# Layer 0's pairs: copying the last product with its bias on ScalarE and adding the residual in one sum

## The chip, the cores and the metric

The kernel runs on one core of a Trainium2 chip. The metric is the device time of one launch in microseconds (us), as the median of several runs. Profiles are of one execution of the same kernel. The engines are named as in the profile: PE (matrix products; PEld is its weight load), DVE (VectorE), ACT (ScalarE), POOL (GpSimd), and SP, which here only issues DMAs. [...]

## The reference, cut to what matters

Sixteen batches of 256 x 256 values pass through two residual layers. Each batch has a router row of eight numbers.

```python
# layer 0: one expert of 8 for each batch, with biases
e = argmax(cond_8, axis=-1)
h = silu(x @ W_up[e].T + b_up[e]) * (x @ W_gate[e].T + b_gate[e])     # 256 -> 512
x = x + (h @ W_down[e].T + b_down[e])                                 # 512 -> 256, residual
# layer 1: the two best experts for each batch, and a shared one; no biases
y = gelu(x @ shared_gate) * (x @ shared_up) @ shared_down             # 256 -> 1024 -> 256
for each of the two experts e with weight w:
    y += w * (gelu(x @ gate[e]) * (x @ up[e]) @ down[e])
x = x + y
```

The change concerns the last line of layer 0: the product with `W_down`, its bias `b_down` and the residual `x`.

## The kernel before, in words

**Units.** Batches are sorted by expert at run time. Two batches with the same expert make a `Pair`, one left over makes a `Single`. In layer 0 there are a first single, one more single, four pairs that always exist (`l0_pairs`), and up to three further pairs or the singles in their place, chosen at run time by a switch. In layer 1 there are the eight shared pairs and the routed ones. The kernel is written with an order by hand: no scheduler moves an instruction within an engine's queue.

**A pair's products** are done as 2 x 2 block products with seven multiplications in place of eight (the list `STEPS`). They need sums of blocks on both sides. On the weight side POOL makes four sums per matrix in `sums_a` (L479 to L482): `sums_q` for each quarter of the first matrices (tile `s`), `sums_d` for the last matrix (tile `ds`). On the activation side DVE makes three instructions in `sums_b` (L472 to L474), for the input `x` (tile `bt` in layer 0, `xt` in layer 1) and for the hidden activations (also in a `bt`). In layer 0 the second of these sums of `x` lies in a `dz` buffer.

**First matrices (`up`, L541).** For each quarter `j`, PE runs the seven products into PSUM banks X, Y and Q. ACT copies X to SBUF (`copy`, L522, tile `cp`), and DVE adds or subtracts Y or Q to or from the copy (`combine`, L526, tile `c`). Then ACT applies the functions: in layer 0 SiLU and an identity, each with bias, in `act0` (L571), in layer 1 the GELU (L577). DVE multiplies the two halves (L580, tile `bt`), and `sums_b` follows. A layer 0 pair has two quarters, a layer 1 pair four.

**Last matrix (`down`, L597).** The seven products go to banks A (for X), B (for Q) and Y. Each of the four result blocks C11, C12, C22, C21 has an `early` and a `late` half. `early` takes the content of A out into a `dz` buffer. In layer 0 that is one DVE instruction which adds the bias column and the block of x (L614). In layer 1 it is an ACT copy with a scale (L619), or for the very last pair a DVE sum (L612). `late` then combines the `dz` buffer with bank Y or B on DVE into the result tile `ys` (L630 where no routing weight is applied). The order in `down` is: after product 0 `early` C11; 1: `late` C11; 2: `early` C12; 4: `early` C22 and C21, `late` C22; 5: `late` C21; 6: `late` C12, and the pair's buffers are given back. Product 2 accumulates into the same bank A that product 0 wrote, so it can start only when the `early` of C11 has read it; product 4 stands likewise behind the `early` of C12.

**Order of the work.** `Line` has a clock that advances with every pair product. `later(after, f)` puts a step off by so many ticks, and `flush` runs what is due. The products of a pair's last matrix are put off and fall among the first products of the next pair. `ahead` runs at the start of each quarter: it loads q five quarters ahead, makes the POOL sums of the first matrices three quarters ahead (`sums_q`), loads the last matrix, and in layer 0 puts that matrix's POOL sums (`sums_d`) off by 12 ticks. A quarter has six products of two ticks each, so 12 ticks is just the next quarter's start.

**Stores.** When a pair is done, `done` records its store and `send` issues it at the start of the next quarter. In layer 0 each of the two batches goes from `ys` to the DRAM tensor `x1d`, from which layer 1 loads its input, and to `out`; both are SP DMAs (L453, L454). `x1d` of the first pair is what layer 1's first shared pair loads into `xt`.

Of the kernel before, what the change touches and what calls it, by code (L numbers as in the profile page):

```python
# [10 lines left out]
AF = mybir.ActivationFunctionType  # L11
ALU = mybir.AluOpType
# [47 lines left out]
def kernel(  # L60
# [10 lines left out]
    nc = tc.nc  # L71
# [40 lines left out]
    def take(tag, *shape, of=None):  # L112

        i = turns[tag].pop(0)
        if tag not in HELD:
            turns[tag].append(i)
        else:
            assert (tag, of) not in turns
            turns[tag, of] = i
        t = rings[tag][i]  # L120
        n = 1
        for d in shape:
            n *= d
        t = t[:, :n]
        if len(shape) == 1:
            return t
        names = "abcd"[: len(shape)]
        return t.rearrange(
            f"p ({' '.join(names)}) -> p {' '.join(names)}", **dict(zip(names, shape))
        )  # L130

    def when_free(tag, f):

        if turns[tag] and not turns["later", tag]:
            f()
        else:
            turns["later", tag].append(f)

    def give(tag, of):
        turns[tag].append(turns.pop((tag, of)))  # L140
        if turns["later", tag]:
            turns["later", tag].pop(0)()

    def bank(tag):
        return take(tag, N2)
# [311 lines left out]

    class Pair(Unit):
        width, last = 2, False
        first, step = 18, None  # L460


# [124 lines left out]
        def down(self, k):  # L587

            tag, a, b = STEPS[k]
            if k == 0:  # L590
                self.ys = take("ys", KD, 2, S, of=self)
            if OPENS[k]:
                self.banks[tag] = bank({"X": "A", "Q": "B", "Y": "Y"}[tag])
            src = self.d[:, A_AT[a]] if a in A_AT else self.ds[:, S_AT[a]]
            d = self.banks[tag][:, :S]
            for j in range(self.kp):
                nc.tensor.matmul(  # L597
                    d,
                    lhsT=src[:, j, :],
                    rhs=self.acts[j][:, B_AT[b], :],  # L600
                    start=OPENS[k] and j == 0,
                    stop=j == self.kp - 1,
                    skip_group_check=True,
                )

            def early(block):
                c, t = block % 2, block // 2
                e = take("dz", S, of=(self, block))
                self.copies[block] = e
                src = self.banks["X"][:, :S]  # L610
                if self.last:
                    nc.vector.tensor_tensor(e, self.z[:, c, t, :], src, ALU.add)  # L612
                elif not self.layer:
                    nc.vector.scalar_tensor_tensor(  # L614
                        e, src, self.bd[:, c : c + 1], self.xt[:, block, :], ALU.add, ALU.add
                    )
                else:
                    w = 1.0 if self.at is None else self.weight(t)
                    nc.scalar.activation(e, src, AF.Copy, scale=w)  # L619

            def late(block, tag, sign):
                c, t = block % 2, block // 2
                e, src = self.copies[block], self.banks[tag][:, :S]
                dst = self.ys[:, c, t, :]
                if self.layer and self.at is not None:
                    nc.vector.scalar_tensor_tensor(  # L626
                        dst, src, self.weight(t, sign), e, ALU.mult, ALU.add
                    )
                else:
                    nc.vector.tensor_tensor(dst, e, src, ALU.add if sign > 0 else ALU.subtract)  # L630
                if self.last:
                    queue = (nc.sync, nc.scalar)[t]
                    store = queue.dma_start(self.out[t][:, c, :], dst)
                    for other in self.stores[1 - t]:
                        tc.declare_no_dep(store.ins, other.ins, reason="another batch")
                    self.stores[t].append(store)
                give("dz", (self, block))

            if k == 0:
                early(C11)  # L640
            elif k == 1:
                late(C11, "Y", 1)
            elif k == 2:
                early(C12)
            elif k == 4:
                early(C22)
                early(C21)
                late(C22, "Q", -1)
            elif k == 5:
                late(C21, "Y", 1)  # L650
            elif k == 6:
                late(C12, "Q", -1)
                give("d", self)
                for j in range(self.kp):
                    give("bt", (self, j))
                if not self.layer:
                    give("bt", self)
                if not self.last:
                    self.done(self.ys)
# [123 lines left out]
    l0_pairs = [Pair(next(names), 0, 2 * i) for i in range(NP1)]  # L783
# [4 lines left out]
    pairs = [Pair(next(names), 1, 2 * i) for i in range(NP2)]  # L788
    more_pairs = [Pair(next(names), 1, 2 * NP2 + 2 * i) for i in range(MOST[1])]
    ones = [Single(next(names), 1, 2 * NP2 + i) for i in range(NS2)]  # L790
    shared[-1].last = True
    shared[-2].step = 7

# [38 lines left out]
    class Line:  # L832
# [24 lines left out]
        def ahead(self, i):  # L857

            at = dict(enumerate(quarters))
            if i + Q_AHEAD in at:  # L860
                u, j = at[i + Q_AHEAD]
                u.load_q(j)
            if i + S_AHEAD in at:
                u, j = at[i + S_AHEAD]
                if u.width == 2:
                    when_free("s", lambda u=u, j=j: u.sums_q(j))
                if j == 0:
                    if u.width == 2 and not u.layer:
                        when_free("bt", u.load_x)
                    else:  # L870
                        if u.layer:
                            self.send(0)
                        u.load_x()
            if i + 1 in at:
                u, j = at[i + 1]
                if u.width == 2 and j == 0:

                    self.later(5 if i > 1 and at[i][0].width == 2 else 0, u.sums_x)
                    self.flush(self.clock)
            if i < 0:  # L880
                return
            u, j = at[i]
            pair0 = u.width == 2 and not u.layer
            if j == 0 and u is not l0_first:
                if u.d_from in HELD:
                    when_free(u.d_from, u.load_d)
                else:
                    u.load_d()
            if pair0 and j:
                self.later(12, u.sums_d)  # L890
            elif u.width == 2 and j == 2:
                u.sums_d()
            if u is shared[-1] and j == 2:
                u.load_z()
# [206 lines left out]
```

## Time and profile before

| what | value |
|---|---|
| median of 3 runs | 1051.06 us (1050.55 to 1051.47) |
| the profiled execution's own time | 1051.36 us |
| its span, first to last instruction | 1049.7 us |
| granted PE clock | 0.999 |
| PE busy, whole span | 1038.2 us |
| DVE busy, whole span | 777.0 us |
| DVE busy from 82 to 112 us (layer 0's pairs) | 28.89 of 30 us |
| ACT busy in the same stretch | 13.11 of 30 us |
| POOL busy in the same stretch | 19.16 of 30 us |
| L614 from 40 to 120 us | 14 instructions, 467 to 485 ns each |

The profile times are of a single execution, in us from the span's start. A row `ys<-dz,Y` reads: writes tile `ys`, from tile `dz` and PSUM bank Y. In a list of waits, each row tells which engine waited at which line for which, the total, the number of waits and the longest. A wait is put down to the release that came last by the profile, which can be a coincidence. In a timeline, the number in brackets is the idle time of the engine ahead of the instruction.

### The profile page before, as it was taken

To read this page: it belongs to the slowest core of one execution; us is meant where nothing else is said; L and a number is where in the kernel's file an instruction comes from. 1 tells how busy PE (TensorE), PEld (TensorE's weight loads), DVE (VectorE), ACT (ScalarE), POOL (GpSimd) and SP (SyncE) were. 2 spreads that over 40 slices of the span, in tenths; PEclk is the share of its full clock that TensorE was granted. 3 is DMA by queue.
4 is the path that set the end of the run, shared out by engine and by line. 5 is a ranking of instruction groups with operands and counts; after the bars stand their busy time and mean duration, and the time that the engine had idled before them with its cause. 6 is when DMAs were issued, how large, how long until landed. Compare 5 with 4: busy or idle time off the path is not lost.

```text
span 1049.7 us, 14152 instructions
## 1 busy us (share of the span) xinstructions
PE 1038.2 (99%) x4750; PEld 900.3 (86%) x4750; DVE 777.0 (74%) x1207; ACT 371.3 (35%) x583; POOL 446.7 (43%) x492
## 2 busy tenths in 40 slices
PE   9999999999999999999999999999999999999998
PEld 6778888888888888888888888888888888888886
DVE  7789978878687877887777778777766236776764
ACT  2444353535333333333333333333333123333331
POOL 2946331221043765666476556645201245630000
PEclk9999999999999999999999999999999999999999
DMA  7636656656664355345335533543655445356522
GB/s 237 241 127 203 240 181 194 207 166 236 200 235 119 88 140 140 93 109 140 98 87 138 140 98 103 140 122 83 178 159 171 133 136 156 91 180 184 183 75 45
DMA packets 60974, 157.47 MB, mean 150 GB/s; under 512 B 7506, under 2 KB 27090, under 8 KB 56658
## 3 DMA queue, kind: packets, MB, share of 16 engines
q1 hardware_dynamic: 47618, 140.90, 40.3%
q0 software_dynamic: 12976, 15.21, 9.4%
q8 instruction: 42, 0.69, 0.3%
q14 instruction: 50, 0.41, 0.1%
q10 hardware_dynamic: 288, 0.26, 0.1%
HBM read 132.23 MB, written 24.12 MB: 149 GB/s over the span
## 4 chain that ended last, share of the span: by engine, by line
PE 89%; DVE 7%; issue 2%; ACT 1%; DMA 1%; SPq 0%; DVEq 0%; ACTq 0%
PE X L541 24%; PE Q L541 16%; PE Y L541 16%; PE A L597 12%; PE B L597 9%; PE Y L597 8%; DVE c L526 2%; PE X L692 2%; PE Q L692 1%; DVE bt L580 1%; PE A L722 1%; DVE bt L472 1%; DVE bt L473 1%; PE B L722 1%; ACT c L577 1%
## 5 line engine op out<-in xcount | busy, mean ns | idle before, releaser
L522 ACT ACTIVATE cp<-X 128x512 f32<-128x512 f32 x318 | 189.5, 596 | 519.2 <-PE X L541 518.6
L580 DVE TENSOR_TENSOR bt<-c 128x1024 f32<-128x1024 f32 x106 | 145.7, 1374 | 102.8 <-ACT c L577 93.0
L541 PE MATMUL Y<-xt,q 128*128 128x256 f32 x736 | 189.8, 380 | 1.1 <-DVE c L526 0.6
L541 PE MATMUL Q<-xt,s 128*128 128x256 f32 x736 | 189.5, 380 | 0.6 <-DVE c L526 0.6
L541 PE MATMUL X<-xt,s 128*128 128x256 f32 x736 | 189.5, 380 | 0.0
L526 DVE TENSOR_TENSOR c<-cp,Q 128x512 f32<-128x512 f32 x212 | 144.3, 681 | 37.4 <-ACT cp L522 32.9
L526 DVE TENSOR_TENSOR c<-cp,Y 128x512 f32<-128x512 f32 x212 | 144.1, 680 | 22.4 <-PE Y L541 22.0
L541 PEld LDWEIGHTS Y<-xt,q 128*128 128x128 f32 x736 | 138.9, 190 | 23.2 <-DVE c L526 3.9
L451 POOL DMA_DIRECT2D out_dram<-ys x46 | 49.0, 1065 | 255.7 <-DVE ys L626 103.2
L541 PEld LDWEIGHTS Q<-xt,s 128*128 128x128 f32 x736 | 139.3, 190 | 21.2 <-DVE c L526 2.5
L541 PEld LDWEIGHTS X<-xt,s 128*128 128x128 f32 x736 | 139.3, 190 | 20.5 <-ACT cp L522 1.4
L479 POOL TENSOR_TENSOR s<-q 128x256 f32<-128x256 f32 x78 | 72.1, 924 | 131.8 <-PE Q L541 66.2
L482 POOL TENSOR_TENSOR s<-s,q 128x256 f32<-128x256 f32 x78 | 62.5, 801 | 101.0 <-PE Q L541 101.0
L597 PE MATMUL A<-bt,ds 128*128 128x256 f32 x424 | 101.5, 379 | 1.4 <-DVE dz L614 1.4
L597 PE MATMUL B<-bt,ds 128*128 128x256 f32 x424 | 101.4, 379 | 0.0
L577 ACT ACTIVATE c<-c 128x1024 f32<-128x1024 f32 x92 | 96.7, 1052 | 12.9 <-DVE c L526 12.7
L472 DVE TENSOR_TENSOR bt<-bt 128x512 f32<-128x512 f32 x113 | 95.0, 840 | 0.7 <-DMA bt<-x_dram 0.6
L541 PE MATMUL X<-xt,q 128*128 128x256 f32 x368 | 94.4, 379 | 0.0
L597 PEld LDWEIGHTS A<-bt,ds 128*128 128x128 f32 x424 | 80.4, 190 | 13.0 <-POOL s L481 1.4
L597 PEld LDWEIGHTS B<-bt,ds 128*128 128x128 f32 x424 | 80.5, 190 | 11.2 <-ACT ys L737 0.3
L597 PE MATMUL Y<-bt,d 128*128 128x256 f32 x376 | 90.0, 379 | 0.0
L597 PEld LDWEIGHTS Y<-bt,d 128*128 128x128 f32 x376 | 71.4, 190 | 9.7
(163 smaller groups left out, 1157.1 us busy)
## 6 DMA issues: line engine op xcount, KB each, us to landing
q<-wq_dram SPq DMA_DIRECT2D x114, 512.0 KB, 3.7
d<-wd_dram SPq DMA_DIRECT2D x22, 1024.0 KB, 6.6
s<-qsums SPq DMA_DIRECT2D x28, 512.0 KB, 4.9
xt<-x1d SPq DMA_DIRECT2D x46, 256.0 KB, 4.3
out_dram<-ys POOLq DMA_DIRECT2D x46, 256.0 KB, 5.1
ds<-dsums SPq DMA_DIRECT2D x7, 1024.0 KB, 6.3
d<-wd_dram SPq DMA_DIRECT2D x7, 513.0 KB, 5.1
bt<-x_dram SPq DMA_DIRECT2D x14, 256.0 KB, 4.7
```

What stands on the lines that cost most here:

```text
L451: nc.gpsimd.dma_start(row(out), ys[:, :, t, :], accum_op=ALU.add)
L472: tt(t[:, 4:6, :], t[:, 0:3:2, :], t[:, 2:4, :], ALU.subtract)
L479: tt(s("S1"), a("A21"), a("A22"), ALU.add)
L482: tt(s("nS4"), s("S2"), a("A12"), ALU.subtract)
L522: nc.scalar.activation(t, self.banks["X", j], AF.Copy)
L526: nc.vector.tensor_tensor(self.c[j][:, block].rearrange("p m s -> p (m s)"), self.copies[n, j], self.banks[tag, j], op,)
L541: nc.tensor.matmul(self.banks[tag, j][:, bass.ts(m, S)], lhsT=self.q[j][:, m, A_AT[a], :] if a in A_AT else self.s[j][:, m, S_AT[a], :], r ...
L577: nc.scalar.activation(u, u, AF.Gelu_apprx_tanh)
L580: nc.vector.tensor_tensor(t[:, 0:4, :], u, v, ALU.mult)
L597: nc.tensor.matmul(d, lhsT=src[:, j, :], rhs=self.acts[j][:, B_AT[b], :], start=OPENS[k] and j == 0, stop=j == self.kp - 1, skip_group_che ...
L692: nc.tensor.matmul(dst[:, bass.ts(half, S)], lhsT=self.q[j][:, m, 2 * half + c, :], rhs=self.xt[:, c, :], start=(c == 0), stop=(c == KD - 1),)
L722: nc.tensor.matmul(self.po[:, bass.ts(c, S)], lhsT=self.d[:, 2 * c + half, j, :], rhs=self.acts[j][:, bass.ts(half, S)], start=(j == 0 and ...
```

## The change

A flag `crowded` is set for the first three of layer 0's four fixed pairs; the fourth and the pairs made at run time stay as they were. For a crowded pair:

- `early` is an ACT instruction, an identity with the bias column of the last matrix, from bank A to the `dz` buffer. It no longer reads x.
- After the last `late`, one DVE tensor_tensor of 128 x 1024 adds the four blocks of x to the whole of `ys`, in place.
- `sums_d` is put off by 14 ticks instead of 12. POOL so makes the sums of the next quarter of first matrices ahead of those of the last matrix.

```diff
     class Pair(Unit):
         width, last = 2, False
+        crowded = False
         first, step = 18, None
...
                 if self.last:
                     nc.vector.tensor_tensor(e, self.z[:, c, t, :], src, ALU.add)
+                elif self.crowded:
+                    nc.scalar.activation(e, src, AF.Identity, bias=self.bd[:, c : c + 1])
                 elif not self.layer:
                     nc.vector.scalar_tensor_tensor(
                         e, src, self.bd[:, c : c + 1], self.xt[:, block, :], ALU.add, ALU.add
...
             elif k == 6:
                 late(C12, "Q", -1)
+                if self.crowded:
+                    ys = self.ys.rearrange("p c t s -> p t c s")
+                    xs = self.xt[:, 0:4, :].rearrange("p (t c) s -> p t c s", t=2)
+                    nc.vector.tensor_tensor(ys, ys, xs, ALU.add)
                 give("d", self)
...
     ones = [Single(next(names), 1, 2 * NP2 + i) for i in range(NS2)]
+    for u in l0_pairs[:-1]:
+        u.crowded = True
...
             if pair0 and j:
-                self.later(12, u.sums_d)
+                self.later(14 if u.crowded else 12, u.sums_d)
```

## The prediction

> **What bounds the kernel now.** I read the page first, then the waits of PE in the stretch of layer 0's pairs (40 to 120 us), then that stretch's timeline.
>
> ```profile
> PE 1038.2 (99%) x4750; PEld 900.3 (86%) x4750; DVE 777.0 (74%) x1207; ACT 371.3 (35%) x583; POOL 446.7 (43%) x492
> ```
>
> PE is busy for all but 11.5 us of a 1049.7 us span, at full clock. An edit to other engines can only win idle PE time, so the question is how much of the 11.5 us lies where the change works. Its three pairs run between about 42 and 118 us.
>
> ```profile
> PE A L597 <- DVE dz L614: 1.4, 2, 1.0
> PE Q L541 <- POOL s L479: 1.2, 1, 1.2
> PE Y L541 <- DVE ys L630: 0.3, 1, 0.3
> PE Q L541 <- DVE c L526: 0.2, 1, 0.2
> ```
>
> The columns are total us, times, longest. It sums to 3.1 us; the first two rows are what the change aims at. The second row's releaser is doubtful. That matmul (51.52 us) accumulates into a bank that a DVE subtraction, `c<-cp,Q`, reads until 51.42 us. POOL's `s` operation of 49.70 us ends at the same moment and serves a later pair. So DVE is the releaser there too. The timeline (start, length, engine, operation, idle before) shows the largest A wait:
>
> ```profile
> 53.32 1.03 PE L597 MATMUL A<-bt,d 128*128 128x256 f32 x4
> ...
> 57.47 0.83 DVE L474 TENSOR_TENSOR bt<-bt,dz 128x256 f32<-128x256 f32 x1
> 58.23 0.47 DVE L614 SCALAR_TENSOR_TENSOR dz<-A,d,bt 128x256 f32<-128x256 f32 x1
> 58.63 1.21 DVE L580 TENSOR_TENSOR bt<-c 128x1024 f32<-128x1024 f32 x1
> 58.85 1.10 PE L597 MATMUL A<-bt,ds 128*128 128x256 f32 x4 [1.05 <-DVE dz L614]
> 59.76 0.67 DVE L526 TENSOR_TENSOR c<-cp,Q 128x512 f32<-128x512 f32 x1
> 60.36 0.41 DVE L630 TENSOR_TENSOR ys<-dz,Y 128x256 f32<-128x256 f32 x1
> 60.81 0.73 PEld L541 LDWEIGHTS Y<-bt,q 128*128 128x128 f32 x4 [0.41 <-DVE ys L630]
> ```
>
> A is complete at 54.35 us, but L614 only runs at 58.23, behind six DVE instructions. The second product into A waits for it. Two matmul groups later PE (its weight load, PEld) waits again, for L630 to free bank Y, on the same DVE queue. One line of the page and four of the timeline show that pair 2's end is different:
>
> ```profile
> DVE  7789978878687877887777778777766236776764
> ```
>
> ```profile
> 111.18 1.28 ACT L577 ACT_TABLE_LOAD   x1
> 112.48 1.06 ACT L577 ACTIVATE c<-c 128x1024 f32<-128x1024 f32 x1
> 113.56 2.29 DVE L580 TENSOR_TENSOR bt<-c 128x1024 f32<-128x1024 f32 x1 [1.59 <-ACT c L577]
> 116.84 1.13 PE L541 MATMUL Y<-xt,q 128*128 128x256 f32 x4 [0.33 <-DVE ys L630]
> ```
>
> The whole-run DVE digits hide the crowd: from 82 to 112 us DVE is busy 28.9 of 30.0 us. Then it idles 1.59 us behind a table load and the first GELU, and PE waits for what follows.
>
> **What the skill says.** The Trainium skill, "SBUF — State Buffer", section "Who interferes with whom": a VectorE instruction with two SBUF inputs and a GpSimd instruction reading SBUF exclude each other for their whole length. The trace agrees: L474 takes 0.42 us with POOL idle (118.87) and 0.83 with POOL busy (57.47). "PSUM — Partial Sum Buffer", section "Engine vs sequencer instructions": ScalarE's, VectorE's and GpSimdE's queues are strict FIFO; L614 above, late behind ready work, agrees.
>
> **The change part by part.** The order of both builds moves exactly this, per pair and for three pairs: four L614 leave DVE, four ACTIVATEs join ACT, one 128x1024 DVE sum comes after the fourth L630, and POOL's four `ds` sums change places with the next four `s` sums. SP's DMAs keep count and order. PE's queue is unchanged.
>
> *Removed from DVE.* L614 takes 0.47 us, 0.40 from start to next start: 4 x 0.40 = 1.6 us a pair.
>
> *Added to DVE.* The sum has two SBUF inputs. Its nearest row is the 128x1024 tensor_tensor of L933, 1.22 us; it also waits for the L630 just before it to drain (the 0.09 us by which L472 to L473 exceeds an overlapped step). I take 1.26 us from step to step. Bounds are 1.2 with POOL idle and 2.3, the L580 above, when it meets POOL. DVE thus loses 0.3 us of work a pair, but the removed pieces and the added piece lie at different places.
>
> *Added to ACT.* Not in the trace with these operands. The nearest are L710 (bias from SBUF, 128x256, 0.47 us) and L619 (Copy, 0.38). "ScalarE: Activation LUTs", section "What ACT_TABLE_LOAD costs", gives 280 + 0.833 x 256 = 493 ns as an estimate. I take 0.47, bounds 0.38 and 0.49. Layer 0 already uses Identity with Silu in L571, and the changed order has no further table load. ACT is 44% busy here, so the time is covered, except where an L571 is queued behind an A product that isn't done.
>
> *Pair 0's A wait (57.8).* ACT can copy A at 54.4, so the 1.05 us goes. Next late is L630 for bank Y: DVE's chain L474, L580, c, L630 is shorter by L614 alone, so Y starts at 60.42, not 60.82: -0.4 us. POOL's new order adds something at 51.5: `s` for the next quarter now comes first, and its fourth sum must wait for PE's read of the old one (until 52.5), so POOL is idle under the L580 at 49.33 (1.49 us, 1.21 alone): up to -0.3. Later POOL meets the L580 at 58.6: up to +0.3. Together about -0.5 us, -0.8 to 0.
>
> *Pair 0's end, pair 1's A (69.75 to 80).* DVE ran without a gap from L630 at 69.75 to L630 at 79.93. It gets +1.26 and -0.40. Two L473/L474 that met POOL (72.1 to 73.7, 0.83 each) lose most of that, since `ds` now comes after `s` and waits for PE at 72.3: -0.6 (0 to -0.8). So DVE ends 79.93 - 0.5 + 0.26 = 79.7, PE starts Y at 79.75 instead of 79.98: PE is now 0.2 us ahead, between 0.8 ahead and 0.5 behind.
>
> *Pairs 1 and 2 (84 to 117).* Four terms. First, L571 at 84.84 is now behind two copies of A, which can't start before 84.57: it starts at 85.5 (84.6 plus two copies), and L580 at 86.8 rather than 86.21, +0.6. Second, two sums, at about 90 and 109: +2.5. Third, four L614 go (94.46, 97.65, two at 102.96), -1.6. Fourth, the two at 102.96 filled a wait: L580 at 104.44 waits for L571, which waits for `c`; without them DVE idles 0.8 more. Sum: +2.3 us when `c` is ready for the GELU, which was at 111.58. The GELU could not start before 112.48, so 0.9 of this is covered by the table load; GELU, L580, c, L630 and PE's Y at 116.84 come 1.4 later. L580 waited for POOL's `ds` sums (2.29 instead of 1.21); starting elsewhere it may win up to 1.0, or meet the next sum just the same. I take +1.2, from +0.2 to +2.3. PE also stops 0.1 to 0.4 us for L630 at 98.2 and 107.7; those are the same lag seen earlier, not added.
>
> *DMAs.* The first x1d store of a pair needed half of its four results and now needs the sum: SP's stores and the loads behind them go 1.3 us (pair 0) and 2.2 us (pair 1) later. xt from x1d landed about 82 and is first read at 92.1 on DVE and 97.4 on PE; q is loaded five quarters ahead. I cost this at nothing. Without that cover it would cost those 1 to 2 us. POOL's moved `ds` are used 15 us and more later: nothing.
>
> *After 118* DVE has room (41.9 busy of 52 us), and PE keeps its shift. Sum: -0.2 + 1.2 = **+1.0 us**. The profiled execution takes 1051.36 us (span 1049.7 and 1.66 around it), 0.30 above the median of 1051.06: 1052.4 on its scale, **1052.1** as a median.
>
> **The rivals.** *A: the stalls really go.* If the L630s keep up, because POOL's new order frees DVE of collisions (eight L473 and L474 of 0.83 in 50 to 80 us, 0.4 each too long), PE wins 1.2 + 1.4 + 0.3 of its 3.1 us less a little: about -2.4, 1048.7. For it: DVE's total falls. Against: the chain of L630s is gapless at 69.75 to 79.93, and 1.26 goes right into it. 10%.
>
> *B: the crowded stretch tips over.* The lag of +2.3 at the GELU grows by the lock: the sum at 90 pushes L472 to L474 from 89.26 to 91.05, into POOL's `ds` sums (91.35 to 95.1), two at +0.4, and the L580 at 113.56 meets POOL again. Then PE's Y at 116.84 is 1.4 + 0.8 + 0.3 = 2.5 later with no gain left from before: 1053.6. It decides from a lag of 3.0 at the GELU. For it: DVE 96% busy at 82 to 112. Against: the collision at 92.8 falls away when the same instructions move past 95. 15%.
>
> *C: it does nothing to PE* (DVE hands every stall on, the A waits turn into equal waits on L630): 1051.1. For it: DVE's work is about the same. Against: the terms above don't cancel at the GELU. 25%, inside the same band as my forecast.
>
> **How the numbers follow.** A measurement of this kernel can tell about 0.2%, 2.1 us, from no change. My forecast has 50% and C 25%; both lie within, 75%. A gives 10% faster, B 15% slower. The range takes in the unknown bounds and half of each rival: 1049.3 to 1053.7.
>
> **What would show it.** Right: PE's A waits for L614 in 57 to 78 us are gone, PE waits for L630 (Y) at about 60 and 80 instead; the new sums take 1.2 to 1.3 us; the first GELU starts about 1.4 us after its table load has ended (0.02 before), and the PE wait after it is above 1 us. Wrong: no wait of PE on L630 before 110 us (A), waits of over 2 us near 117 (B), or any ACT-bound wait of PE.

## The result, and the profile after

| | before | changed |
|---|---|---|
| median | 1051.24 us (6 runs) | 1056.95 us (6 runs, 1055.92 to 1057.97) |
| ratio to before, 95% interval | | 1.0058 (1.0048 to 1.0069) |
| profiled execution: own time, span | 1051.36, 1049.7 us | 1057.84, 1056.2 us |
| granted PE clock | 0.999 | 1.000 |

The change makes the kernel 5.7 us slower. The forecast was 1052.1 us, within 1049.3 to 1053.7, with 15% for "slower". The time lies outside the range.

In the changed kernel's code the lines stand a little lower: `combine` is L527 (was L526), `up` L542, `down` L598, SiLU L572, GELU L578, the product of the halves L581, the sums of `sums_b` L473 to L475, POOL's four sums L480 to L483, the new ACT copy L615, the old DVE form of it L617, `late` L633. The new residual sum is L659, and the line that makes `z` is L943 (was L933).

One line of the page, the busy times of the whole run:

```profile
PE 1037.9 (98%) x4750; PEld 899.7 (85%) x4750; DVE 777.2 (74%) x1198; ACT 376.0 (36%) x595; POOL 446.9 (42%) x492
```

It says little. Twelve L614 of 0.47 us went (5.7 us), three sums of 1.22 came (3.7 us), and DVE's busy time should have fallen by 2 us; it rose by 0.2. So other DVE instructions became longer. Which ones, only a timeline can tell. The waits of PE from 40 to 180 us (total us, times, longest):

```profile
PE Y L542 <- DVE ys L633: 5.6, 4, 2.7
PE Y L542 <- DVE c L527: 1.1, 1, 1.1
PE Q L542 <- issue: 0.9, 1, 0.9
PE Q L542 <- DVE c L527: 0.2, 1, 0.2
```

They sum to 7.8 us, against 3.1 before. The two waits for `dz` in bank A are gone, as planned, and five waits for bank Y stand in their place. PE's timeline gives their places (start, length, operation, idle before):

```profile
51.20 1.10 PE L542 MATMUL Q<-bt,s 128*128 128x256 f32 x4 [0.88 <-issue]
59.96 1.13 PE L542 MATMUL Y<-bt,q 128*128 128x256 f32 x4 [0.75 <-DVE ys L633]
81.35 1.13 PE L542 MATMUL Y<-bt,q 128*128 128x256 f32 x4 [2.70 <-DVE ys L633]
101.05 1.13 PE L542 MATMUL Y<-xt,q 128*128 128x256 f32 x4 [1.30 <-DVE ys L633]
117.96 1.13 PE L542 MATMUL Y<-xt,q 128*128 128x256 f32 x4 [1.10 <-DVE c L527]
121.83 1.13 PE L542 MATMUL Y<-xt,q 128*128 128x256 f32 x4 [0.83 <-DVE ys L633]
```

Against the same matmuls before, PE is 0.32 us ahead at 51.20, 0.86 ahead at 59.96, 1.37 behind at 81.35, 2.83 behind at 101.05 (2.94 one group later), and 4.99 behind at 121.83. So each of the three sums is followed by a loss. After that the gap stays near 5 us until 180 us. The rest, up to 6.4 at the end of this pair of executions, is scattered over small waits, most of them for DVE.

What happens between a sum and the next loss is seen after the first sum. First DVE in the kernel before, from the last `late` of pair 0 to the one that frees bank Y:

```profile
69.75 0.42 DVE L630 TENSOR_TENSOR ys<-dz,B 128x256 f32<-128x256 f32 x1 [0.17 <-PE B L597]
...
71.34 0.69 DVE L472 TENSOR_TENSOR bt<-bt 128x512 f32<-128x512 f32 x1
72.07 0.83 DVE L473 TENSOR_TENSOR bt<-bt 128x256 f32<-128x256 f32 x1
72.94 0.83 DVE L474 TENSOR_TENSOR bt<-bt 128x256 f32<-128x256 f32 x1
...
79.52 0.41 DVE L630 TENSOR_TENSOR ys<-dz,Y 128x256 f32<-128x256 f32 x1
```

Then the changed kernel, DVE and POOL together:

```profile
69.35 1.22 DVE L659 TENSOR_TENSOR ys<-ys,bt 128x1024 f32<-128x1024 f32 x1
...
70.49 1.22 DVE L581 TENSOR_TENSOR bt<-c 128x1024 f32<-128x1024 f32 x1
...
71.74 1.12 DVE L473 TENSOR_TENSOR bt<-bt 128x512 f32<-128x512 f32 x1
...
72.63 0.59 POOL L496 DMA_DIRECT2D qsums<-s  x1 [0.31 <-POOL s L483]
72.90 1.37 DVE L474 TENSOR_TENSOR bt<-bt 128x256 f32<-128x256 f32 x1
...
73.24 0.74 POOL L480 TENSOR_TENSOR ds<-d 128x256 f32<-128x256 f32 x1
...
74.06 0.80 POOL L481 TENSOR_TENSOR ds<-ds,d 128x256 f32<-128x256 f32 x1
...
74.31 0.83 DVE L475 TENSOR_TENSOR bt<-bt 128x256 f32<-128x256 f32 x1
...
78.62 1.74 DVE L581 TENSOR_TENSOR bt<-c 128x1024 f32<-128x1024 f32 x1
...
80.89 0.41 DVE L633 TENSOR_TENSOR ys<-dz,Y 128x256 f32<-128x256 f32 x1
```

The sum itself takes what was forecast, 1.22 us. But L473, L474 and L475 behind it now run 1.12, 1.37 and 0.83 us, together 0.97 more than before, and the L581 at 78.62 takes 1.74 where it took 1.35. They run beside POOL's work on `s` and `ds`. Before, the stretch from the last `late` of pair 0 (start at 69.75) to the L630 that frees bank Y (start at 79.52) took 9.77 us; now it takes 12.00, from 68.89 to 80.89. PE waits 2.70 us at the end of it.

### The profile page after: what moved, and what is told of

Read it like the earlier page. It is cut to its first block, busy times and chain, and to the rows that moved or that the text cites. A ratio compares the mean times of both kernels' runs of the same rounds, so it can differ in the third digit from the quotient of the medians.

```text
span 1056.2 us, 14139 instructions
## 1 busy us (share of the span) xinstructions
PE 1037.9 (98%) x4750; PEld 899.7 (85%) x4750; DVE 777.2 (74%) x1198; ACT 376.0 (36%) x595; POOL 446.9 (42%) x492
## 4 chain that ended last, share of the span: by engine, by line
PE 85%; DVE 9%; issue 2%; ACT 1%; POOL 1%; DMA 1%; SPq 0%; DVEq 0%; ACTq 0%; POOLq 0%
PE X L542 22%; PE Q L542 15%; PE Y L542 15%; PE A L598 12%; PE B L598 9%; PE Y L598 7%; DVE c L527 3%; DVE bt L581 2%; PE X L699 2%; PE Q L699 1%; DVE bt L473 1%; PE A L729 1%; DVE bt L474 1%; ACT c L578 1%; PE B L729 1%
## 5 line engine op out<-in xcount | busy, mean ns | idle before, releaser
L581 DVE TENSOR_TENSOR bt<-c 128x1024 f32<-128x1024 f32 x106 | 147.1, 1388 | 105.0 <-ACT c L578 94.1
L542 PE MATMUL Y<-xt,q 128*128 128x256 f32 x736 | 190.1, 381 | 4.6 <-DVE c L527 2.4
L542 PE MATMUL Q<-xt,s 128*128 128x256 f32 x736 | 189.5, 380 | 0.7 <-DVE c L527 0.7
L542 PE MATMUL X<-xt,s 128*128 128x256 f32 x736 | 189.5, 380 | 0.2 <-ACT cp L523 0.2
L527 DVE TENSOR_TENSOR c<-cp,Q 128x512 f32<-128x512 f32 x212 | 144.2, 680 | 38.0 <-ACT cp L523 33.1
L542 PEld LDWEIGHTS Y<-xt,q 128*128 128x128 f32 x736 | 138.8, 190 | 27.7 <-DVE c L527 6.3
L527 DVE TENSOR_TENSOR c<-cp,Y 128x512 f32<-128x512 f32 x212 | 144.0, 679 | 22.8 <-PE Y L542 22.4
L542 PEld LDWEIGHTS Q<-xt,s 128*128 128x128 f32 x736 | 139.3, 190 | 21.3 <-DVE c L527 2.6
L542 PEld LDWEIGHTS X<-xt,s 128*128 128x128 f32 x736 | 139.3, 190 | 20.8 <-ACT cp L523 1.7
L480 POOL TENSOR_TENSOR s<-q 128x256 f32<-128x256 f32 x78 | 70.0, 898 | 132.5 <-PE Q L542 64.0
L483 POOL TENSOR_TENSOR s<-s,q 128x256 f32<-128x256 f32 x78 | 60.1, 771 | 110.9 <-PE Q L542 110.9
L578 ACT ACTIVATE c<-c 128x1024 f32<-128x1024 f32 x92 | 96.7, 1051 | 17.0 <-DVE c L527 17.0
L598 PE MATMUL B<-bt,ds 128*128 128x256 f32 x424 | 101.4, 379 | 0.0
L598 PE MATMUL A<-bt,ds 128*128 128x256 f32 x424 | 101.4, 379 | 0.0
L473 DVE TENSOR_TENSOR bt<-bt 128x512 f32<-128x512 f32 x113 | 97.6, 864 | 0.4 <-DMA bt<-x_dram 0.3
L542 PE MATMUL X<-xt,q 128*128 128x256 f32 x368 | 94.4, 379 | 0.0
L598 PEld LDWEIGHTS A<-bt,ds 128*128 128x128 f32 x424 | 80.5, 190 | 11.2 <-issue 0.3
L598 PEld LDWEIGHTS B<-bt,ds 128*128 128x128 f32 x424 | 80.5, 190 | 11.2 <-ACT ys L744 0.3
L598 PE MATMUL Y<-bt,d 128*128 128x256 f32 x376 | 90.0, 379 | 0.0
L481 POOL TENSOR_TENSOR s<-s,q 128x256 f32<-128x256 f32 x78 | 79.1, 1014 | 6.1
```

The lines of the kernel that those rows point to most:

```text
L473: tt(t[:, 4:6, :], t[:, 0:3:2, :], t[:, 2:4, :], ALU.subtract)
L480: tt(s("S1"), a("A21"), a("A22"), ALU.add)
L481: tt(s("S2"), s("S1"), a("A11"), ALU.subtract)
L483: tt(s("nS4"), s("S2"), a("A12"), ALU.subtract)
L527: nc.vector.tensor_tensor(self.c[j][:, block].rearrange("p m s -> p (m s)"), self.copies[n, j], self.banks[tag, j], op,)
L542: nc.tensor.matmul(self.banks[tag, j][:, bass.ts(m, S)], lhsT=self.q[j][:, m, A_AT[a], :] if a in A_AT else self.s[j][:, m, S_AT[a], :], r ...
```

## The experiments

From the traces I had two theories at first. **P**: POOL's new order (`sums_d` at 14 ticks) puts its work under DVE's. **S**: the residual sum does it, whatever POOL's order. Within S two readings stood against each other later. **M**: a sum costs more than its own length, since it moves the instructions behind it into POOL's sums. **L**: only its length counts. Each round's times are given with the median of before taken on the same chip.

**First round: the three parts apart** (before: 1050.86 us).

The changed kernel with POOL's old order:

```diff
-                self.later(14 if u.crowded else 12, u.sums_d)
+                self.later(12, u.sums_d)
```

> The changed kernel with `sums_d` put off by 12 ticks again: copies on ACT and the sum stay, POOL's order is that of before. Theory P (POOL's new order puts its sums under DVE's gapless stretches, and the exclusion makes DVE wait): the DVE stretch of 69 to 81 us loses 1 to 1.4 us of its longer L473, L474 and L581, pair 2's stretch stays as it was; in all 3 to 4 us above the kernel before instead of 5.7. Theory S (the sum itself, put where DVE has no gap, is the cost; POOL only decides which instruction waits): 5 to 6 us above.

Measured: 1056.89 us, ratio 1.0051 (1.0035 to 1.0068). As slow as the change: P falls.

The kernel before with POOL's new order and nothing else:

```diff
-                self.later(12, u.sums_d)
+                self.later(14 if u in l0_pairs[:-1] else 12, u.sums_d)
```

> The kernel before with only `sums_d` of the first three pairs put off by 14 ticks. Theory P: DVE's stretch 69 to 80 us collides in other places, +0.5 to +1.5 us, and PE's wait at 51.5 us gets 0.3 shorter: 0 to +1.2 us in all. Theory S: nothing but the 0.3 us: -0.5 to 0.

Measured: 1049.90 us, ratio 0.9989 (0.9980 to 0.9997), 1.0 us below its before, which is lower than either theory named. The new order alone costs nothing, and may win a little.

The changed kernel without the residual sum (its result lacks `x` for the three pairs):

```diff
-                if self.crowded:
-                    ys = self.ys.rearrange("p c t s -> p t c s")
-                    xs = self.xt[:, 0:4, :].rearrange("p (t c) s -> p t c s", t=2)
-                    nc.vector.tensor_tensor(ys, ys, xs, ALU.add)
```

> The changed kernel with the residual sum left out for the three pairs (so x is missing from their result): the copies on ACT and POOL's new order stay. Theory P: the collisions remain, so PE still waits for L633 at about 80 us, 0.5 to 1 us; in all between -0.5 and +1 us against before. Theory S: all of the loss goes and the gain at 57.8 us stays: -0.8 to -2 us.

Measured: 1050.40 us, ratio 0.9995 (0.9987 to 1.0004). And the same with POOL's old order, so the copies on ACT alone:

> The copies on ACT alone: no residual sum (x missing from the result of three pairs), POOL's order as before. Theory P: -1 to -2 us, better than the same with POOL's new order by 1 us or more. Theory S: -0.8 to -2 us, the same as with POOL's new order within 0.4. A third theory, that the copies hold back the activations behind them on ACT: 0 to +1.

Measured: 1050.45 us, ratio 0.9998 (0.9989 to 1.0007).

With the changed kernel these make a square. Taking the sum away wins 6.4 us in POOL's old order (1056.89 - 1050.45) and 6.2 in the new one (5.7 above its before against 0.5 below). The sums' own length is 3 x 1.22 = 3.7 us. So S holds for the cost: it is the sum, in either order of POOL. The sums cost some 1.7 times their length. S's figures for the kernels without the sum do not hold: they lie 0.5 and 0.4 us below their before, where S named 0.8 to 2. That shortfall would allow the third theory, that the copies hold back the activations behind them on ACT, a share that these runs don't separate. The second finding is that 4.8 us of L614 (three pairs, four each, 0.40 apiece) taken off DVE win nothing that can be told from no change. The timeline without the sum, over the stretch shown above:

```profile
70.45 0.69 DVE L473 TENSOR_TENSOR bt<-bt 128x512 f32<-128x512 f32 x1
71.18 0.42 DVE L474 TENSOR_TENSOR bt<-bt 128x256 f32<-128x256 f32 x1
...
71.64 0.93 DVE L475 TENSOR_TENSOR bt<-bt 128x256 f32<-128x256 f32 x1
...
73.21 0.74 POOL L480 TENSOR_TENSOR ds<-d 128x256 f32<-128x256 f32 x1
...
78.90 1.13 PE L542 MATMUL Y<-bt,q 128*128 128x256 f32 x4 [0.58 <-DVE ys L633]
```

The same three instructions take 2.04 us instead of 3.32: they are through before POOL's first `ds` sum at 73.21, and only L475 meets an `s` sum (71.56 to 72.29). PE's Y starts at 78.90 instead of 81.35: a sum of 1.22 us made it 2.45 later.

**Second round: length against place** (before: 1051.19 us).

The sum cut into four, each 128x256 directly after its block's `late`, in place of the one at the end:

```diff
                 else:
                     nc.vector.tensor_tensor(dst, e, src, ALU.add if sign > 0 else ALU.subtract)
+                if self.crowded:
+                    nc.vector.tensor_tensor(dst, dst, self.xt[:, block, :], ALU.add)
```

> The changed kernel with the one 128x1024 sum cut into four of 128x256, each right after its block's L633. Theory M (the sum costs more than its length because it moves the instructions behind it into POOL's sums, and stands in one piece in a stretch without gaps): two of the four pieces fall where DVE waits for ACT's copies of A, so most of the loss goes, +0.5 to +2.5 us against before. Theory L (DVE's added length alone decides, 1.26 us a sum, pieces are no shorter: 4 x 0.42 and more): still +4 to +6.

Measured: 1054.51 us, ratio 1.0033 (1.0021 to 1.0046). It is 3.3 us above its before: more than M's range, less than L's. Spreading the sum saves 2.4 us of the change's loss, though four short sums are longer together than one (4 x 0.42 us against 1.22). In its trace PE is level with before from 84 to 107 us and loses 2.7 at the third pair's end, where L475 (1.38 us) and `z` (2.28) still meet POOL's sums.

The changed kernel without POOL's four `ds` sums for the third and fourth pair (those products then read stale `ds`):

```diff
-            self.sums_a(lambda n: d[:, A_AT[n]], lambda n: s[:, S_AT[n]])
+            if self not in l0_pairs[2:]:
+                self.sums_a(lambda n: d[:, A_AT[n]], lambda n: s[:, S_AT[n]])
```

> The changed kernel without POOL's four `ds` sums for the third and the fourth pair (these two use the buffers of the first two pairs, so their results are not the reference's). Those sums lie at 73 to 76 and 92 to 95 us, under L473 to L475 after the first and the second residual sum. Theory M: DVE's lag after the first sum falls by 0.8 to 1.3 us, after the second by 0.8 to 1.4; in all 1.5 to 3 us below the changed kernel. Theory L: at most 0.5 below it.

Measured: 1053.49 us, ratio 1.0023 (1.0014 to 1.0032), 2.3 us above its before where the change is 5.7 above. That is 3.4 us saved, far from L's 0.5 and above the 3 that M named at most. Its timeline, DVE and POOL, again behind the first sum:

```profile
71.56 0.72 POOL L483 TENSOR_TENSOR s<-s,q 128x256 f32<-128x256 f32 x1 [3.89 <-PE Q L543]
71.72 1.12 DVE L473 TENSOR_TENSOR bt<-bt 128x512 f32<-128x512 f32 x1
72.60 0.59 POOL L496 DMA_DIRECT2D qsums<-s  x1 [0.31 <-POOL s L483]
72.87 0.43 DVE L474 TENSOR_TENSOR bt<-bt 128x256 f32<-128x256 f32 x1
73.33 0.42 DVE L475 TENSOR_TENSOR bt<-bt 128x256 f32<-128x256 f32 x1
```

L474 and L475 are short again at the late place. Of POOL's work only the DMA issue of 72.60 is left beside them, and L474 takes 0.43 within it. So it was POOL's `ds` sums that stretched them; L473 meets the `s` sum of 71.56 and stays long. The same edit on the kernel before:

> The kernel before without the same `ds` sums of POOL (third and fourth pair, results not the reference's): what collisions with these sums cost where there is no residual sum. Both theories: PE's waits at 77.9 and 80 us (about 1 us with the restarts) go in part: 0 to -1 us. If it gains as much as the same edit in the changed kernel, the exclusion isn't what the residual sum costs extra.

Measured: 1050.69 us, ratio 1.0001 (0.9992 to 1.0009). So the same POOL sums cost 3.4 us with the residual sums in DVE's queue, and 0.5 or nothing without them. That is M, for the sums left out here, which stand behind the first and the second residual sum. Behind the third stand the `ds` sums of layer 1's first pair, which no run takes away.

As an attempt at a better version, POOL's new order and only the first block C11 on ACT, with its own 128x256 add behind its `late`:

```diff
                 if self.last:
                     nc.vector.tensor_tensor(e, self.z[:, c, t, :], src, ALU.add)
+                elif self in l0_pairs[:-1] and block == C11:
+                    nc.scalar.activation(e, src, AF.Identity, bias=self.bd[:, c : c + 1])
...
                     nc.vector.tensor_tensor(dst, e, src, ALU.add if sign > 0 else ALU.subtract)
+                if self in l0_pairs[:-1] and block == C11:
+                    nc.vector.tensor_tensor(dst, dst, self.xt[:, block, :], ALU.add)
...
-                self.later(12, u.sums_d)
+                self.later(14 if u in l0_pairs[:-1] else 12, u.sums_d)
```

> POOL's new order as in the run with that alone, and of the four blocks only C11, the one whose copy PE waits for (0.37 and 0.20 us left there), is copied by ACT; its x is added on DVE (128x256) right after its L633. The other blocks keep L614. Theory M: DVE's length is about the same, PE's two waits on A go, and bank Y comes 0.4 us earlier: -1 to -2 us against before, 0 to 0.8 below POOL's order alone. Theory L: the same or up to 0.3 above POOL's order alone.

Measured: 1050.44 us, ratio 0.9997 (0.9988 to 1.0005), 0.8 us below its before where POOL's order alone was 1.0 below. So it is no better; M's forecast missed here, and the time is what L named. PE's waits show what happened. First POOL's order alone, then with the C11 copy, from 40 to 126 us (rows that both have are left out):

```profile
PE A L597 <- DVE dz L614: 0.6, 2, 0.4
```

```profile
PE Y L541 <- DVE ys L632: 1.3, 2, 0.7
```

The copy takes away two waits on bank A, and PE meets two on bank Y two matmul groups later. It starts the first of these Y products at 59.92 us, and at 59.91 with POOL's order alone: what DVE has queued ahead of bank Y sets that time, not the instruction that was moved.

**Third round: the sums one at a time** (before: 1050.55 us, for the last run 1051.03). Always with POOL's new order for all three pairs; `crowded` is set for one pair only, and the others add `x` in `early` on DVE as before. The edit for the first pair (`[2:3]` for the third, `[1:2]` for the second):

```diff
-    for u in l0_pairs[:-1]:
+    for u in l0_pairs[:1]:
         u.crowded = True
...
-                self.later(14 if u.crowded else 12, u.sums_d)
+                self.later(14 if u in l0_pairs[:-1] else 12, u.sums_d)
```

The base, POOL's order alone, once more:

> The kernel before with nothing but POOL's order changed, once more, beside e9 and e10 on the same chip, as their base and as the fastest version found: 0.5 to 1.4 us below the kernel before, a ratio near 0.999 whose interval leaves out 1.

Measured: 1050.13 us, ratio 0.9999 (0.9990 to 1.0007). The gain of the first round did not repeat. In both traces PE is 1.7 us ahead of before at 119 us, but no gain can be claimed from the times.

> The changed kernel with the copies on ScalarE and the residual sum for the first pair alone; POOL's order stays changed for all three pairs, and the second and third pair add the residual in their early copies again. Theory M (a sum costs more than its length, because it pushes the instructions behind it into POOL's sums): the first sum costs TensorE what the trace without the sum showed between the two second products of the second pair, 78.90 against 81.35 us, so 2.2 to 2.5 us above the kernel with POOL's order alone (1049.9): 1051.9 to 1052.4. Theory L (the added length alone): 1.26 us above it less a little for the shorter early copies, 1050.7 to 1051.2.

Measured: 1052.35 us, ratio 1.0020 (1.0012 to 1.0027), 2.2 above the base, in M's range and outside L's.

> The same for the third pair alone. Theory M: the sum at about 106 us on the clock of the kernel before pushes L475 and z (L943) into POOL's 128x512 ds sums, and bank Y is read late before the last pair's first GELU: 2 to 3 us above POOL's order alone, 1051.9 to 1052.9. Without the first two sums' delay everything comes some 3 us earlier against POOL's ds sums, whose start hangs on loads: if the overlap goes with that, the third sum costs 1 us or less, and its cost in the changed kernel was passed on by the first two. Theory L: 1.26 us, 1051.2.

Measured: 1053.11 us, ratio 1.0027 (1.0015 to 1.0039), 3.0 above the base and just above M's range; the alternative that the third cost was handed on by the first two is out. This is the clearest pair of traces, as both run at the same times up to the sum. First the base, then with the third sum alone:

```profile
106.80 0.69 DVE L472 TENSOR_TENSOR bt<-bt 128x512 f32<-128x512 f32 x1
...
107.52 0.42 DVE L473 TENSOR_TENSOR bt<-bt 128x256 f32<-128x256 f32 x1
107.98 0.42 DVE L474 TENSOR_TENSOR bt<-bt 128x256 f32<-128x256 f32 x1
108.32 1.22 DVE L933 TENSOR_TENSOR z<-ats 128x1024 f32<-128x1024 f32 x1
...
110.09 1.27 POOL L479 TENSOR_TENSOR ds<-d 128x512 f32<-128x512 f32 x1
110.65 0.48 DVE L614 SCALAR_TENSOR_TENSOR dz<-A,d,bt 128x256 f32<-128x256 f32 x1
```

```profile
106.92 1.28 DVE L659 TENSOR_TENSOR ys<-ys,bt 128x1024 f32<-128x1024 f32 x1
108.12 0.68 DVE L473 TENSOR_TENSOR bt<-bt 128x512 f32<-128x512 f32 x1
...
108.84 0.83 DVE L474 TENSOR_TENSOR bt<-bt 128x256 f32<-128x256 f32 x1
109.42 1.38 POOL L480 TENSOR_TENSOR ds<-d 128x512 f32<-128x512 f32 x1
...
109.71 1.38 DVE L475 TENSOR_TENSOR bt<-bt 128x256 f32<-128x256 f32 x1
110.88 1.33 POOL L481 TENSOR_TENSOR ds<-ds,d 128x512 f32<-128x512 f32 x1
111.01 2.28 DVE L943 TENSOR_TENSOR z<-ats 128x1024 f32<-128x1024 f32 x1
112.17 2.25 POOL L482 TENSOR_TENSOR ds<-d 128x512 f32<-128x512 f32 x1
...
114.41 0.47 DVE L617 SCALAR_TENSOR_TENSOR dz<-A,d,bt 128x256 f32<-128x256 f32 x1
```

In the base the whole row, `z` included, is done at 109.54, half a microsecond before POOL begins its 128x512 `ds` sums. From the start of the first row to the last `dz<-A` it takes 3.85 us. With the sum ahead of it, it takes 7.49 from the sum's start: 1.20 for the sum, and 0.41, 0.96 and 1.06 more for L474, L475 and `z`, which sums to 3.6, the whole of what it is longer. A sum of 1.2 us pushes its followers over an edge and costs DVE three times itself.

> The same for the second pair alone. If the three sums' costs add up, theory M with the measured 2.2 us for the first and 3.0 for the third leaves 6.5 - 5.2 = 1.3 us for the second, a ratio to the kernel before of about 1.001 (0.4 to 2.2 us above POOL's order alone). The sum's own length is 1.2 us, so the second would then cost about its length and no more. Under theory L every pair costs the same: 1.3 here too, which can't tell the theories apart; a ratio of 1.002 or more would say that the second sum also moves work into POOL's sums, and that the three together cost less than one by one.

Measured: 1051.57 us, ratio 1.0001 (0.9993 to 1.0009). Set against its own before it is 0.5 us up where the base is 0.4 down, so the second sum costs about 1.0, a little under the 1.3 named and no more than its own length. Its followers are stretched too in its trace (L473 1.26 us, L474 and L475 0.83 each), and PE waits 1.50 us at 97.55. At 119 us PE is 1.3 us behind before in this trace, where the base is 1.7 ahead. Only 0.5 of that stands already at 40 us, so the trace shows a larger cost than the times do. This execution was the slowest of its 13 (1052.54 us), and the difference stays open. By the times, then, M's excess shows at the first and the third sum. One by one the sums cost 2.2 + 1.0 + 3.0 = 6.2 us over the base. The change, 5.7 above its before, stands 6.1 above the base. So they add up, within the 1 us or so that these intervals leave.

## Why the prediction was wrong, point by point

**The new operations' lengths were right.** Sum 1.22 to 1.23 us (taken: 1.22, 1.26 from step to step), ACT copy 0.46 to 0.47 (taken: 0.47; the 0.493 worked out beside it was a little too long), no further table load, no wait of PE on ACT from 40 to 180 us. The later stores cost nothing to be seen: PE waits for no DMA there.

**Pair 0's A wait: right in kind, a little small.** Forecast -0.5 us (at most -0.8), measured -0.86 at PE's Y at 59.96. The wait moved from A to Y, as said (0.75 us on L633). The wait at 51.5 shrank from 1.22 to 0.88, close to the 0.3 that was put down to the collision at 49.33, and that product of the halves now takes 1.25 us where it took 1.49.

**Pair 0's end: the step that failed.** The term was +1.26 for the sum, -0.40 for L614 and -0.6 "relief", since L473 and L474 "lose most of" their collisions when `ds` comes after `s`. The relief was real only without the sum: there L474 takes 0.42, and the three take 2.04 us against 2.35. The step that failed is this relief. The prediction laid the moved `ds` over DVE's old times, 72.1 to 73.7, although its own first number put those instructions 1.26 later, straight into the `ds` sums that start at 73.24. In place of -0.6 stood +1.37: the stretch grew by 2.23 (9.77 to 12.00), of which the sum and L614 explain 0.86, the longer L473 to L475 0.97, and the longer L581 0.39. PE's Y came 1.37 late where 0.2 early was forecast.

**Pairs 1 and 2: right list, one term missing.** The +0.6 for L571 behind two copies came as about +0.5: the L581 at 88.06, released by L572, starts 1.85 us later than before, of which 1.37 is PE's lag by then. DVE idles 1.16 us ahead of it, where it was 0.35. "Two sums, +2.5" was their own length only. Behind the second sum L473 to L475 became 1.22, 0.83 and 0.83 us (0.68, 0.42, 0.42 before), +1.36. Behind the third stood `z`, which the prediction used as a measure of length but never placed. It took 1.22 us before and was through before POOL's `ds` sums; after the change it meets them (2.29 us at 115.02), so that `c` is late for the GELU, as two lines of ACT show:

```profile
114.11 1.28 ACT L578 ACT_TABLE_LOAD   x1
...
118.53 1.06 ACT L578 ACTIVATE c<-c 128x1024 f32<-128x1024 f32 x1 [3.13 <-DVE c L527]
```

The lag when `c` is ready was forecast as 2.3 us and measured 6.9 (118.50 against 111.58). The GELU starts 6.05 later than before, 3.1 after the end of its table load, where 1.4 was forecast. The term was +1.2 us on PE and measured 3.6 (1.37 behind at 81.35, 4.99 at 121.83).

**The bound was drawn round the wrong thing.** For the sum it stood at 1.2 to 2.3 us, "when it meets POOL". The sum never met POOL for long (0.2 us at the second, where POOL starts at 92.22). Its followers did, and they were not in the bound. Pair 0's own bound, at worst 0.5 behind, was broken by 0.9.

**The rivals.** B had the mechanism, the sum pushing L472 to L474 into POOL's `ds` sums, but at one place of three, with +0.8 for it, and its counter-argument (the collision at 92.8 falls away) held for one instruction: L474 at 97.10 takes 0.42 where it took 0.83, against 1.36 more for L473 to L475 ahead of it. It gave 1053.6 and 15%. A (the stalls really go) failed: no gain that the times can tell came from the removed L614, with the sum or without it. C (stalls handed on) is what the copies alone do: 1050.45 us, and the two A waits (1.4 us) have become two Y waits (1.7).

**A rule quoted and then not applied forward.** The Trainium skill, "SBUF — State Buffer", section "Who interferes with whom", says that a VectorE instruction with two SBUF inputs contends with a GpSimd instruction that reads SBUF. The traces agree that one of the two is held up. Where it is DVE, its 128x256 takes up to 1.38 us against 0.42 alone, and its 128x1024 up to 2.29 against 1.22. Where it is POOL, DVE keeps its time: the L581 at 107.76 of the changed kernel takes 1.23, and the POOL sum that starts at 107.80 takes 1.77, against 0.73 alone. The prediction used the rule to explain rows of the old trace and not to place the rows of the new one.

**What stays open.** Whether POOL's order alone wins anything (0.9989 once, 0.9999 once). No version here is shown to beat the kernel before. That POOL's `ds` sums stretch `z` behind the third sum is read from a pair of traces, without a run that leaves them out. The 1.4 us between PE's lag at 122 us (5.0) and at the end of the two profiled executions (6.4) was not followed up.

## What to carry to other kernels

When an instruction is put into a queue that has no gap, price not only its length but everything that it pushes: lay the queue's following instructions at their new times over the other engine that holds them up (here POOL), before counting any relief. Look for the instruction that ends just ahead of the other engine's burst, here `z` with half a microsecond to spare, because that is where 1.2 us become 3.6. And work taken off a busy engine is a gain only if the stall does not come back at the next thing that the same queue has to deliver: 4.8 us of removed DVE work moved PE's stall from one bank to the next and won nothing that could be measured.

## What the runs showed of the hardware that was not expected

L474 took 1.37 us at 72.90, more than the 0.83 of its usual collisions. Ahead of it POOL issued a DMA (72.63 to 73.22), and L480 (0.74) ran until 73.98. The DMA issue does not hold such an instruction: without POOL's `ds` sums it stood there as before (72.60 to 73.19), and L474 took 0.43 us within it. So the `ds` sum held it. L474 ends 0.29 us after that sum, just as L475 at 109.71 of the third-pair trace ends 0.29 after the POOL sum of 109.42. Why it had to wait for a sum that is recorded as starting 0.34 later than itself, no run shows.

In the profiled execution of the changed kernel with POOL's old order, PE slowed down after a wait of 2.43 us for bank Y. PE busy time (and count), granted clock, DMA share and GB/s in short windows:

```profile
82.00:83.00 1.00, 1.00 (x5) 0.72 0.66 262
83.00:84.00 1.00, 1.00 (x4) 0.50 0.08 33
84.00:85.00 1.00, 1.00 (x3) 0.50 0.00 0
85.00:86.00 1.00, 1.00 (x4) 0.58 0.00 0
```

The clock was at half for about 3.4 us (0.56 + 1 + 1 + 0.84, if it was either 0.5 or 1), which by this estimate costs 1.7 us of PE's work; this execution took 1058.43 us, 1.5 above the median of its kernel. The Trainium skill, "TensorE: Matmul & The Clock Gate", section "Part 1: The HAM clock gate (the "warmup" mystery)", tells of such a half-rate state after an idle window of some 3.4 us that runs freely. The length agrees; the idle time doesn't, as PE had waited only 2.43 us, and the measurement decides. The changed kernel's profile has a longer wait, 2.70 us, and no such dip. So this wait of PE cost more than itself in one execution; how often that happens, these runs don't tell.
